# Two last groups of a four-layer graph network by halves, and a planner's costs for small GpSimd operations and loads

## The chip, the cores and the metric

The kernel runs on one core of a Trainium2 chip. The core has five engines that run side by side, each with a queue of its own which it works off in order: TensorE (PE, matmuls), VectorE (DVE), ScalarE (ACT), GpSimd (POOL) and SyncE (SP, which here only starts transfers). The metric is the time of one execution on the device in microseconds; the median of several runs stands for a kernel.

## What is computed

128 graphs of 64 nodes with 256 features each pass four layers. Each layer normalises its input, applies ReLU, runs a graph operation and adds the result to x.

```python
def layer0(h):                       # graph convolution twice, then LSTMs over windows of nodes
    h = relu(adj @ (h @ Wg0 + bg0)); h = relu(adj @ (h @ Wg1 + bg1))
    for p in 1, 2, 3, 4:             # windows of p nodes; the last node of each takes the LSTM's state
        last = lstm_last(Wih[p-1], Whh[p-1], bih[p-1], bhh[p-1], windows(h, p))
        h = h.at[:, arange(64 // p) * p + p - 1].set(last)
    return h
def layer1(x, L):                    # L scaled by its largest eigenvalue; attention; MLP
    x1 = relu(layernorm((L_norm @ x) @ Wc + bc, g1, be1)) + x
    x2 = layernorm(x1 + attention(x1, Wq, Wk, Wv) @ Wo + bo, g2, be2)
    return layernorm(x2 + gelu(x2 @ W1 + b1) @ W2 + b2, g3, be3)
def layer2(h):                       # graph attention: e[i,j] = leaky_relu(s1[i] + s2[j])
    Wh = h @ W; e = leaky_relu((Wh @ a1)[:, :, None] + (Wh @ a2)[:, None, :], 0.2)
    return softmax(where(adj == 0, -inf, e)) @ Wh
def layer3(f):                       # U: eigenvectors of the normalised Laplacian (eigh)
    h = relu((U.T @ f) @ W1 + b1)
    return U @ (h @ W2 + b2)
for layer in layers: x = x + layer(relu(layernorm(x)))
```

## The kernel before

Rows of x (128 graphs x 64 nodes) are cut into 64 tiles of 128 rows, two graphs in each. Layer 0 works on 8 groups of 8 tiles and writes its result to a scratch array in DRAM (`put`). Layers 1 to 3 work on 16 groups of 4 tiles (`HT = 4`), which the loop at the end of the kernel fetches from there (`fetch`), passes through `layer1`, `layer2`, `layer3` and stores by two tiles. The eigenvectors are computed beside layer 0 by a long row of small operations on 64 partitions, mostly on VectorE.

No instruction is issued as it is written. `plan.proxy` records each call as an `Op` with the engine, its dependencies, and a cost and latency by formula (`cost`); `Plan.schedule` then goes through time: at each step it takes the operation that can start first, gives it a buffer from a pool (`big`, `stat`, `bank` and others) and advances its engine's clock, and `Plan.issue` emits everything in the order found. So all instructions of the profile have one line, L347, that of the emitting loop, and groups are told apart by the names of tiles. A tile's name is that of the memory it was given: `sums`, `mids`, `arena`, `Wih` and `Whh` are reused as working buffers once their first use is over. The planner's clock shapes the order alone; on the chip an instruction starts when its semaphores allow.

What the change touches in the planner:

- In `record`, `op.port` marks operations [...] all of GpSimd's, and VectorE's with all operands in SBUF that are no reductions or statistics.
- In `cost`, the branch for `"G"` gives a GpSimd operation its duration: a power 0.44 + 0.14 n us, others 0.12 + 0.00218 n, where n is the elements of a partition.
- In `schedule`, the clock `port` is held for the operation's whole cost, and no operation with `op.port` may start in the plan before it is free. A dependent operation is ready at the end of the one before it plus `slack`: 0.4 us for a TensorE operation of the later layers, 0.12 for other TensorE operations, 0.05 otherwise.
- `rank` orders what could start at once. The last six groups share one rank level and then go by group and by the length of the path behind them.

Of the layers, these steps recur in the argument. `ln_stats` takes statistics of each tile on VectorE (`bn_stats`, `bn_aggr`), then four GpSimd operations on 128x4 values, one of them the power -0.5. `relu_norm` applies them on ScalarE, tile by tile. `mix` multiplies each tile's two graphs by a 64x64 matrix with small matmuls into two banks, which ScalarE copies out (`mix_fm`). `layer2` forms the scores from two weighted sums (`scalar_tensor_tensor` with `accum_out`), a matmul that spreads s2 over rows (`s2d`), six steps on 128x256 values, an exponential, a transpose, the mix by the attention, the product by `W2a` and a scaled add to x. `layer3` mixes by `Ub`, multiplies by `W3a`, takes the maximum with the negated bias, mixes by `UTb`, adds `C3`, multiplies by `W3b` and adds to x.

Of the kernel before, what the change touches and what calls it, by code (L numbers as in the profile page):

```python
# [12 lines left out]
N = 64  # L13
# [55 lines left out]
class Plan:  # L69
# [44 lines left out]
    def record(self, eng, name, args, kw):  # L114
# [42 lines left out]
        if op is self.run:  # L157
# [5 lines left out]
                                 and all(str(ap.space) == "SB" for ap in flat))  # L163
        op.index = len(self.ops)
# [14 lines left out]
    def cost(op, aps):  # L179
# [39 lines left out]
        if op.eng == "G":  # L219
            c = 0.44 + 0.14 * n if op.kw.get("op") is ALU.pow else 0.12 + 0.00218 * n  # L220
            return c, c + 0.05
# [8 lines left out]
    def schedule(self):  # L230
# [20 lines left out]
        while len(order) < len(self.ops):  # L251
# [42 lines left out]
            if op.port:  # L294
                port = t + cost
# [13 lines left out]
            for o in op.after:  # L309
                o.wait -= 1  # L310
                if o.eng != e:
                    o.ready = max(o.ready, end + self.slack(o))
                else:
                    o.ready = max(o.ready, end - 0.01 if op in o.late and e != "PE" else t + cost)
                if not o.wait:
                    ready[o.eng].append(o)
# [577 lines left out]
P = 128  # L894
# [116 lines left out]
def gnn_kernel(ctx: ExitStack, tc: tile.TileContext, a, out):  # L1011
# [54 lines left out]
    def bank(name):  # L1066
        return plan.value("bank")
# [541 lines left out]
    def relu_norm(x):  # L1609
        sc, bi = ln_stats(x)  # L1610
        h = tm()
        for t in range(HT):
            ACT.activation(h[:, t, :], x[:, t, :], AF.Relu, scale=sc(t), bias=bi(t))
        return h

    def mix_fm(h, m):

        dst = fm()
        for i, ps in enumerate(mix(lambda t, c: h[:, t, tok(c)], m, HT)):
            evac(dst.rearrange("p c (t b n) -> p c t b n", t=HT, b=2)[:, :, :, i, :], ps, 1)  # L1620
        return dst
# [76 lines left out]
    def layer2(x):  # L1698


        h = relu_norm(x)
        big, stat = plan.value("big"), plan.value("stat")
        s12 = stat[:, 2 * HT:4 * HT].rearrange("p (k t) -> p k t", k=2)
        for k in range(2):
            for t in range(HT):
                V.scalar_tensor_tensor(big[:, t * D:(t + 1) * D], h[:, t, :], 1.0, wa[:, k, :], op0=ALU.mult, op1=ALU.mult, accum_out=s12[:, k, t:t + 1])

        s2d, s1m, e2, e = (big[:, i * HT * N:(i + 1) * HT * N].rearrange("p (t n) -> p t n", n=N) for i in range(4))
        V.tensor_mul(s2d, vec(ident2), s12[:, 1, :].unsqueeze(2).to_broadcast([P, HT, N]))
        G.tensor_add(s1m, vec(mask2), s12[:, 0, :].unsqueeze(2).to_broadcast([P, HT, N]))  # L1710
        ps = bank("s2")[:, :HT * N]
        PE.matmul(ps, same, flat(s2d), start=True, stop=True)
        V.tensor_add(flat(e), ps, flat(s1m))
        V.tensor_scalar(e2, e, 0.2, None, op0=ALU.mult)
        V.tensor_max(e, e, e2)
        softmax_shift(e, stat[:, :HT])
        attn = plan.value("attn").rearrange("p (t k) -> p t k", t=HT)
        for i in range(2):
            r = half(i)
            ACT.activation(attn[r, :, r], e[r], AF.Exp)  # L1720
        ssum = stat[:, HT:2 * HT]
        V.reduce_sum(ssum, attn, axis=AX.X)
        V.reciprocal(ssum, ssum)
        pT = plan.value("big")[:, :HT * P]
        evac(pT, transposes([attn[:, t, :] for t in range(HT)]), 1)
        aT = mix_fm(h, lambda t: pT[:, tok(t)])
        for t0 in (0, 2):
            ps = proj_tm(lambda c, t: aT[:, c, tok(t)], W2a, 2, t0)
            for t in (t0, t0 + 1):
                V.scalar_tensor_tensor(x[:, t, :], ps[:, (t - t0) * D:(t - t0 + 1) * D], ssum[:, t:t + 1], x[:, t, :], op0=ALU.mult, op1=ALU.add)  # L1730

    def layer3(x):
        h = relu_norm(x)
        for t0 in (0, 2):
            G.tensor_add(x[:, t0:t0 + 2, :], x[:, t0:t0 + 2, :], vec(b3b, 2))
        aT = mix_fm(h, lambda t: Ub)
        hid = tm(HT, P)
        ps = bank("hid")
        for t in range(HT):
            for c in range(2):  # L1740
                PE.matmul(ps[:, tok(t)], aT[:, c, tok(t)], W3a[:, c, :], start=c == 0, stop=c == 1)
        V.tensor_tensor(hid, ps.rearrange("p (t f) -> p t f", t=HT), vec(nb3a), op=ALU.max)
        uT = tm(HT, P)
        for i, ps in enumerate(mix(lambda t, c: hid[:, t, :], lambda t: UTb, HT, 1)):
            V.tensor_tensor(uT.rearrange("p t (b n) -> p t b n", b=2)[:, :, i, :], ps[:, 0], vec(C3[:, half(i)]), op=ALU.add)
        for t0 in (0, 2):
            ps = proj_tm(lambda c, t: uT[:, t, :], W3b.unsqueeze(1), 1, t0)
            V.tensor_add(pair(x, t0), ps, pair(x, t0))

    for g in range(NT // HT):  # L1750
        plan.group = REST + g
        x = fetch(put[g // 2][:, g % 2 * HT:(g % 2 + 1) * HT])
        layer1(x)
        layer2(x)
        layer3(x)
        for t0 in range(0, HT, 2):
            SP.dma_start(xout[g][:, t0:t0 + 2, :], x[:, t0:t0 + 2, :])
# [54 lines left out]
```

## Time and profile before

| | us |
|---|---|
| median of 3 runs | 2116.32 |
| lowest, highest | 2113.99, 2117.18 |
| the profiled execution | 2117.02 |
| its span, first to last instruction | 2115.2 |
| mean granted TensorE clock | 0.997 |
| 256 KB stores, issue to landing (median) | 2.6 |
| 512 KB fetches from `put` to `big` (median) | 6.4 |

In the profile, PE is the matmul stream and PEld the loading of its weights; a float32 matmul leaves two MATMUL and two LDWEIGHTS records. A line of a timeline gives start, duration, engine, line, operation, output and inputs, shapes, how many equal instructions were merged (x4), and in brackets how long the engine had been idle before and what released it. The granted clock is TensorE's, 1.00 at full speed. In time the stages lie so: layer 0 with the eigenvectors up to about 1240 us, a change-over in which its last group and the first groups of the later layers run together, then the later layers, the last six groups interleaved.

### The profile page before, as it was taken

What the parts mean: (1) busy time and instruction counts of PE and PEld (TensorE: products, weight loads), DVE (VectorE), ACT (ScalarE), POOL (GpSimd) and SP (SyncE); (2) the same over time, 40 slices, a digit from 0 to 9 for tenths busy, and PEclk for the clock granted to TensorE, in tenths of its full rate; (3) what the DMA queues carried; (4) which work ended last, traced back from release to release, by engine and by line L of the source; (5) the groups of instructions that cost most, each with busy time, mean ns of one, the idle gap of its engine ahead of it and who ended that gap; (6) DMA issues with size and microseconds to landing.
All of it is one profiled execution on the core that took longest, in us unless ns stands there. A gap on an engine that the chain in (4) does not pass through costs nothing.

```text
span 2115.2 us, 48093 instructions
## 1 busy us (share of the span) xinstructions
PE 2072.3 (98%) x17924; PEld 1675.9 (79%) x17924; DVE 1767.0 (84%) x6669; ACT 1094.7 (52%) x2451; POOL 756.6 (36%) x1144
## 2 busy tenths in 40 slices
PE   8999999999999999999999999999999999999997
PEld 6688689688788788788788789877778778877775
DVE  7788888889999999999988956868779699885785
ACT  3344544534543543543444345666666567575763
POOL 6522212222201201201100215685467658663452
PEclk9999999999999999999999999999999999999999
DMA  6000100100100100100000211100000000000001
GB/s 229 1 3 13 52 3 2 62 2 2 60 1 1 61 1 2 46 1 10 32 1 21 90 49 35 62 1 22 22 21 22 21 22 22 22 2 11 1 12 51
DMA packets 44875, 57.83 MB, mean 27 GB/s; under 512 B 8929, under 2 KB 38497, under 8 KB 44641
## 3 DMA queue, kind: packets, MB, share of 16 engines
q1 hardware_dynamic: 43536, 53.71, 7.9%
q8 instruction: 141, 2.31, 0.5%
q10 hardware_dynamic: 1104, 1.05, 0.2%
q14 instruction: 94, 0.76, 0.1%
HBM read 37.53 MB, written 16.78 MB: 26 GB/s over the span
## 4 chain that ended last, share of the span: by engine, by line
PE 80%; DVE 13%; issue 2%; ACT 2%; POOL 2%; DMA 0%; SPq 0%; ACTq 0%; DVEq 0%; POOLq 0%
PE bank L347 64%; PE seed L347 16%; DVE arena L347 5%; DVE big L347 4%; DVE stat L347 2%; ACT mids L347 1%; DVE mids L347 1%; POOL stat L347 1%; DVE sums L347 1%; POOL big L347 1%; ACT big L347 0%; DMA arena<-put 0%; DVE bank L347 0%; POOL sums L347 0%; DVE seed L347 0%
## 5 line engine op out<-in xcount | busy, mean ns | idle before, releaser
L347 PE MATMUL bank<-big,Wih 128*128 128x512 f32 (+4 forms) x1802 | 554.5, 424 | 2.9 <-DVE big L347 1.9
L347 PEld LDWEIGHTS bank<-big,Wih 128*128 128x128 f32 x1802 | 314.7, 190 | 145.5 <-issue 95.5
L347 PE MATMUL bank<-big,sums 128*128 128x128 f32 (+3 forms) x2328 | 375.7, 289 | 5.2 <-DVE seed L347 2.5
L347 ACT ACTIVATE mids<-bank,bl 128x512 f32<-128x512 f32 (+2 forms) x432 | 247.2, 576 | 214.3 <-PE bank L347 195.2
L347 PEld LDWEIGHTS bank<-big,sums 128*128 128x128 f32 (+1 forms) x2328 | 298.5, 180 | 42.8 <-issue 19.6
L347 PE MATMUL bank<-big,Whh 128*128 128x128 f32 (+3 forms) x1294 | 312.3, 327 | 0.0
L347 DVE TENSOR_TENSOR arena<-arena 64x42 f32<-64x42 f32 (+6 forms) x1358 | 276.5, 231 | 18.4 <-POOL arena L347 1.2
L347 PEld LDWEIGHTS bank<-big,Whh 128*128 128x128 f32 x1294 | 214.0, 191 | 18.5 <-issue 10.5
L347 ACT ACTIVATE mids<-seed,bl 128x256 f32<-128x256 f32 (+2 forms) x192 | 102.0, 531 | 217.0 <-PE seed L347 209.0
L347 DVE TENSOR_TENSOR big<-mids 128x512 f32<-128x512 f32 (+2 forms) x256 | 151.1, 597 | 27.1 <-ACT mids L347 17.1
L347 POOL TENSOR_SCALAR stat<-stat 128x4 f32<-128x4 f32 (+1 forms) x228 | 68.4, 301 | 281.1 <-DVE stat L347 268.9
L347 PE MATMUL seed<-big,sums 128*128 128x128 f32 (+3 forms) x896 | 143.3, 291 | 0.0
L347 DVE SCALAR_TENSOR_TENSOR arena<-arena 64x1 f32<-64x1 f32 (+15 forms) x565 | 136.1, 264 | 4.5 <-POOL arena L347 1.0
L347 POOL TENSOR_TENSOR big<-big 128x128 f32<-128x128 f32 (+2 forms) x55 | 32.9, 600 | 294.6 <-DVE big L347 151.7
L347 POOL TENSOR_TENSOR stat<-stat,mhalf 128x4 f32<-128x4 f32 (+1 forms) x114 | 123.9, 1087 | 4.8
L347 ACT COPY seed<-bank 128x128 f32<-128x128 f32 (+2 forms) x192 | 54.0, 281 | 135.8 <-PE bank L347 128.5
L347 ACT ACTIVATE mids<-big 128x256 f32<-128x256 f32 (+2 forms) x176 | 89.5, 511 | 66.3 <-DVE big L347 62.1
L347 ACT COPY mids<-bank 128x256 f32<-128x256 f32 (+3 forms) x290 | 94.8, 352 | 51.9 <-PE bank L347 51.5
L347 PEld LDWEIGHTS seed<-big,sums 128*128 128x128 f32 (+1 forms) x896 | 118.4, 183 | 3.5 <-issue 0.3
L347 DVE TENSOR_SCALAR arena<-arena 64x1 f32<-64x1 f32 (+10 forms) x506 | 100.4, 206 | 7.8 <-POOL arena L347 0.5
L347 DVE TENSOR_TENSOR big<-big,mids 128x256 f32<-128x256 f32 (+2 forms) x196 | 99.0, 509 | 7.0 <-ACT mids L347 6.0
L347 PE MATMUL bank<-Wih,big 128*128 128x256 f32 x408 | 104.8, 383 | 0.0
(517 smaller groups left out, 4480.4 us busy)
## 6 DMA issues: line engine op xcount, KB each, us to landing
big<-in_x_dram SPq DMA_DIRECT2D x29, 512.0 KB, 5.0
put<-big SPq DMA_DIRECT2D x15, 512.0 KB, 3.2
big<-put SPq DMA_DIRECT2D x8, 512.0 KB, 6.4
out_dram<-big SPq DMA_DIRECT2D x16, 256.0 KB, 2.6
Wih<-in_WihT_dram SPq DMA_DIRECT2D x3, 1024.0 KB, 11.4
Whh<-in_WhhT_dram SPq DMA_DIRECT2D x3, 1024.0 KB, 12.9
arena<-put SPq DMA_DIRECT2D x3, 512.0 KB, 5.9
sums<-put SPq DMA_DIRECT2D x3, 512.0 KB, 4.3
```

The costliest lines, as they stand in the source:

```text
L347: getattr(self.engines[op.eng], name)(*map(real, args), **{k: real(a) for k, a in kw.items()})
```

## The change

`layer2` and `layer3` take a step: 4 tiles as before for the first 14 groups, 2 tiles for the last two. With a step of 2 each passes through its whole row of operations for tiles 0 and 1 and again for tiles 2 and 3, in shared buffers (`h`, `aT` and others) but with statistics and score values of its own. In the planner three costs change: an operation whose operands all have two dimensions and at most 64 elements in a row holds the port for 0.06 us instead of its whole cost; a GpSimd operation of at most 64 elements other than a power costs 0.2 us; and whatever depends on a transfer that SP started is held ready 1.5 us later. These three bear on the order of the whole kernel.

```diff
@@ -161,6 +161,8 @@
 
         op.port = eng == "G" or (eng == "V" and not name.startswith("bn_") and "reduce" not in name
                                  and all(str(ap.space) == "SB" for ap in flat))
+        wide = max(ap.ap[-1][1] if len(ap.ap) == 2 else 65 for ap in flat) > 64
+        op.hold = op.cost if wide else 0.06
         op.index = len(self.ops)
         self.ops.append(op)
         self.link(op)
@@ -217,7 +219,7 @@
                 c += 0.12
             return c, c + 0.15
         if op.eng == "G":
-            c = 0.44 + 0.14 * n if op.kw.get("op") is ALU.pow else 0.12 + 0.00218 * n
+            c = 0.44 + 0.14 * n if op.kw.get("op") is ALU.pow else 0.12 + 0.00218 * n if n > 64 else 0.2
             return c, c + 0.05
         c = max(0.6, free(aps[0]) * aps[0].ap[0][1] * 4e-6 / 0.39)
         return c, c + 2.2
@@ -292,7 +294,7 @@
                 many, cost, lat = op.many, cost + 0.178, lat + 0.178
             now[e] = t + cost
             if op.port:
-                port = t + cost
+                port = t + min(cost, op.hold)
             end = t + lat
             for v in op.vals:
                 if v.buf is None:
@@ -309,7 +311,7 @@
             for o in op.after:
                 o.wait -= 1
                 if o.eng != e:
-                    o.ready = max(o.ready, end + self.slack(o))
+                    o.ready = max(o.ready, end + self.slack(o) + (1.5 if e == "SP" else 0.0))
                 else:
                     o.ready = max(o.ready, end - 0.01 if op in o.late and e != "PE" else t + cost)
                 if not o.wait:
@@ -1606,18 +1608,19 @@
         V.reduce_max(mx, s, axis=AX.X)
         V.tensor_sub(s, s, mx.unsqueeze(2).to_broadcast(list(s.shape)))
 
-    def relu_norm(x):
-        sc, bi = ln_stats(x)
-        h = tm()
-        for t in range(HT):
-            ACT.activation(h[:, t, :], x[:, t, :], AF.Relu, scale=sc(t), bias=bi(t))
+    def relu_norm(x, h=None, t0=0, n=HT):
+        h = tm() if h is None else h
+        sc, bi = ln_stats(x[:, t0:t0 + n], n)
+        for t in range(n):
+            ACT.activation(h[:, t0 + t, :], x[:, t0 + t, :], AF.Relu, scale=sc(t), bias=bi(t))
         return h
 
-    def mix_fm(h, m):
-
-        dst = fm()
-        for i, ps in enumerate(mix(lambda t, c: h[:, t, tok(c)], m, HT)):
-            evac(dst.rearrange("p c (t b n) -> p c t b n", t=HT, b=2)[:, :, :, i, :], ps, 1)
+    def mix_fm(h, m, dst=None, t0=0, n=HT):
+
+        dst = fm() if dst is None else dst
+        part = dst[:, :, t0 * P:(t0 + n) * P].rearrange("p c (t b n) -> p c t b n", t=n, b=2)
+        for i, ps in enumerate(mix(lambda t, c: h[:, t0 + t, tok(c)], lambda t: m(t0 + t), n)):
+            evac(part[:, :, :, i, :], ps, 1)
         return dst
 
     def layer1(x):
@@ -1695,64 +1698,70 @@
             V.tensor_mul(x2[:, t0:t0 + 2, :], x2[:, t0:t0 + 2, :], vec(g3, 2))
             V.tensor_add(x[:, t0:t0 + 2, :], x[:, t0:t0 + 2, :], x2[:, t0:t0 + 2, :])
 
-    def layer2(x):
-
-
-        h = relu_norm(x)
-        big, stat = plan.value("big"), plan.value("stat")
-        s12 = stat[:, 2 * HT:4 * HT].rearrange("p (k t) -> p k t", k=2)
-        for k in range(2):
-            for t in range(HT):
-                V.scalar_tensor_tensor(big[:, t * D:(t + 1) * D], h[:, t, :], 1.0, wa[:, k, :], op0=ALU.mult, op1=ALU.mult, accum_out=s12[:, k, t:t + 1])
-
-        s2d, s1m, e2, e = (big[:, i * HT * N:(i + 1) * HT * N].rearrange("p (t n) -> p t n", n=N) for i in range(4))
-        V.tensor_mul(s2d, vec(ident2), s12[:, 1, :].unsqueeze(2).to_broadcast([P, HT, N]))
-        G.tensor_add(s1m, vec(mask2), s12[:, 0, :].unsqueeze(2).to_broadcast([P, HT, N]))
-        ps = bank("s2")[:, :HT * N]
-        PE.matmul(ps, same, flat(s2d), start=True, stop=True)
-        V.tensor_add(flat(e), ps, flat(s1m))
-        V.tensor_scalar(e2, e, 0.2, None, op0=ALU.mult)
-        V.tensor_max(e, e, e2)
-        softmax_shift(e, stat[:, :HT])
-        attn = plan.value("attn").rearrange("p (t k) -> p t k", t=HT)
-        for i in range(2):
-            r = half(i)
-            ACT.activation(attn[r, :, r], e[r], AF.Exp)
-        ssum = stat[:, HT:2 * HT]
-        V.reduce_sum(ssum, attn, axis=AX.X)
-        V.reciprocal(ssum, ssum)
-        pT = plan.value("big")[:, :HT * P]
-        evac(pT, transposes([attn[:, t, :] for t in range(HT)]), 1)
-        aT = mix_fm(h, lambda t: pT[:, tok(t)])
-        for t0 in (0, 2):
-            ps = proj_tm(lambda c, t: aT[:, c, tok(t)], W2a, 2, t0)
-            for t in (t0, t0 + 1):
-                V.scalar_tensor_tensor(x[:, t, :], ps[:, (t - t0) * D:(t - t0 + 1) * D], ssum[:, t:t + 1], x[:, t, :], op0=ALU.mult, op1=ALU.add)
-
-    def layer3(x):
-        h = relu_norm(x)
-        for t0 in (0, 2):
-            G.tensor_add(x[:, t0:t0 + 2, :], x[:, t0:t0 + 2, :], vec(b3b, 2))
-        aT = mix_fm(h, lambda t: Ub)
-        hid = tm(HT, P)
-        ps = bank("hid")
-        for t in range(HT):
-            for c in range(2):
-                PE.matmul(ps[:, tok(t)], aT[:, c, tok(t)], W3a[:, c, :], start=c == 0, stop=c == 1)
-        V.tensor_tensor(hid, ps.rearrange("p (t f) -> p t f", t=HT), vec(nb3a), op=ALU.max)
-        uT = tm(HT, P)
-        for i, ps in enumerate(mix(lambda t, c: hid[:, t, :], lambda t: UTb, HT, 1)):
-            V.tensor_tensor(uT.rearrange("p t (b n) -> p t b n", b=2)[:, :, i, :], ps[:, 0], vec(C3[:, half(i)]), op=ALU.add)
-        for t0 in (0, 2):
-            ps = proj_tm(lambda c, t: uT[:, t, :], W3b.unsqueeze(1), 1, t0)
-            V.tensor_add(pair(x, t0), ps, pair(x, t0))
+    def layer2(x, step):
+
+        h, big, attn = tm(), plan.value("big"), plan.value("attn").rearrange("p (t k) -> p t k", t=HT)
+        pT, aT = plan.value("big")[:, :HT * P], fm()
+        for t0 in range(0, HT, step):
+            n, ts = step, slice(t0, t0 + step)
+            relu_norm(x, h, t0, n)
+            stat = plan.value("stat")
+            s12 = stat[:, 2 * HT:2 * HT + 2 * n].rearrange("p (k t) -> p k t", k=2)
+            for k in range(2):
+                for t in range(n):
+                    V.scalar_tensor_tensor(big[:, (t0 + t) * D:(t0 + t + 1) * D], h[:, t0 + t, :], 1.0, wa[:, k, :], op0=ALU.mult, op1=ALU.mult, accum_out=s12[:, k, t:t + 1])
+
+            s2d, s1m, e2, e = (big[:, (t0 * 4 + i * n) * N:(t0 * 4 + (i + 1) * n) * N].rearrange("p (t n) -> p t n", n=N) for i in range(4))
+            V.tensor_mul(s2d, vec(ident2, n), s12[:, 1, :].unsqueeze(2).to_broadcast([P, n, N]))
+            G.tensor_add(s1m, vec(mask2, n), s12[:, 0, :].unsqueeze(2).to_broadcast([P, n, N]))
+            ps = bank("s2")[:, :n * N]
+            PE.matmul(ps, same, flat(s2d), start=True, stop=True)
+            V.tensor_add(flat(e), ps, flat(s1m))
+            V.tensor_scalar(e2, e, 0.2, None, op0=ALU.mult)
+            V.tensor_max(e, e, e2)
+            softmax_shift(e, stat[:, :n])
+            for i in range(2):
+                r = half(i)
+                ACT.activation(attn[r, ts, r], e[r], AF.Exp)
+            ssum = stat[:, HT:HT + n]
+            V.reduce_sum(ssum, attn[:, ts], axis=AX.X)
+            V.reciprocal(ssum, ssum)
+            pt = bank("tr")
+            for t in range(n):
+                PE.transpose(pt[:, tok(t)], attn[:, t0 + t, :], ident)
+            evac(pT[:, t0 * P:(t0 + n) * P], pt[:, :n * P], 1)
+            mix_fm(h, lambda t: pT[:, tok(t)], aT, t0, n)
+            for u0 in range(t0, t0 + n, 2):
+                ps = proj_tm(lambda c, t: aT[:, c, tok(t)], W2a, 2, u0)
+                for t in (u0, u0 + 1):
+                    V.scalar_tensor_tensor(x[:, t, :], ps[:, (t - u0) * D:(t - u0 + 1) * D], ssum[:, t - t0:t - t0 + 1], x[:, t, :], op0=ALU.mult, op1=ALU.add)
+
+    def layer3(x, step):
+        h, aT, hid, uT = tm(), fm(), tm(HT, P), tm(HT, P)
+        for t0 in range(0, HT, step):
+            n, ts = step, slice(t0, t0 + step)
+            relu_norm(x, h, t0, n)
+            for u0 in range(t0, t0 + n, 2):
+                G.tensor_add(x[:, u0:u0 + 2, :], x[:, u0:u0 + 2, :], vec(b3b, 2))
+            mix_fm(h, lambda t: Ub, aT, t0, n)
+            ps = bank("hid")
+            for t in range(n):
+                for c in range(2):
+                    PE.matmul(ps[:, tok(t)], aT[:, c, tok(t0 + t)], W3a[:, c, :], start=c == 0, stop=c == 1)
+            V.tensor_tensor(hid[:, ts], ps[:, :n * P].rearrange("p (t f) -> p t f", t=n), vec(nb3a, n), op=ALU.max)
+            for i, ps in enumerate(mix(lambda t, c: hid[:, t0 + t, :], lambda t: UTb, n, 1)):
+                V.tensor_tensor(uT[:, ts].rearrange("p t (b n) -> p t b n", b=2)[:, :, i, :], ps[:, 0], vec(C3[:, half(i)], n), op=ALU.add)
+            for u0 in range(t0, t0 + n, 2):
+                ps = proj_tm(lambda c, t: uT[:, t, :], W3b.unsqueeze(1), 1, u0)
+                V.tensor_add(pair(x, u0), ps, pair(x, u0))
 
     for g in range(NT // HT):
         plan.group = REST + g
         x = fetch(put[g // 2][:, g % 2 * HT:(g % 2 + 1) * HT])
         layer1(x)
-        layer2(x)
-        layer3(x)
+        step = 2 if g >= NT // HT - 2 else HT
+        layer2(x, step)
+        layer3(x, step)
         for t0 in range(0, HT, 2):
             SP.dma_start(xout[g][:, t0:t0 + 2, :], x[:, t0:t0 + 2, :])
     plan.issue()
```

## The prediction

> **What bounds the kernel now.** I read the page first (busy shares, slices), then busy time by stage, then the timeline of the last chain, then the releasers.
>
> ```profile
> span 2115.2 us, 48093 instructions
> PE 2072.3 (98%) x17924; PEld 1675.9 (79%) x17924; DVE 1767.0 (84%) x6669; ACT 1094.7 (52%) x2451; POOL 756.6 (36%) x1144
> PE   8999999999999999999999999999999999999997
> ```
>
> TensorE is busy 98%, and its slices are all nines but the first and the last. So only its idle time, 2115.2 - 2072.3 = 42.9 us, and work done at a lowered clock can be won. Where that lies, the busy time by stage says (columns: stretch, length, then busy time and count of each engine, granted clock, DMA share, GB/s):
>
> ```profile
> 0.00:16.00 16.00, 12.28 (x92) 10.45 (x96) 9.61 (x62) 5.10 (x9) 7.01 (x29) 0.79 0.81 255
> 106.00:1216.00 1110.00, 1104.84 (x7637) 902.18 (x7636) 1004.83 (x4403) 506.36 (x1297) 196.66 (x369) 1.00 0.07 22
> 1216.00:1428.00 212.00, 204.45 (x1843) 180.30 (x1842) 143.27 (x398) 120.81 (x270) 112.08 (x149) 1.00 0.12 36
> 1428.00:2062.00 634.00, 625.58 (x7009) 496.53 (x7007) 507.54 (x1449) 412.80 (x767) 368.83 (x502) 1.00 0.05 17
> 2062.00:2092.45 30.45, 24.29 (x422) 20.83 (x423) 22.90 (x75) 13.13 (x27) 11.05 (x17) 1.00 0.16 54
> 2092.45:2111.40 18.95, 13.01 (x173) 9.88 (x171) 7.87 (x21) 3.15 (x6) 4.18 (x6) 0.83 0.09 29
> 2111.40:2115.20 3.80, 0.00 (x0) 0.00 (x0) 0.69 (x1) 0.00 (x0) 0.00 (x0) 0.94 0.42 138
> ```
>
> TensorE idles 3.7 us up to 16, 5.2 in the 1110 us of layer 0, 7.6 where layer 0 gives way to the later layers, 8.4 in the next 634, then 6.2 in 30, 5.9 in 19, and 3.8 at the very end, where one add and the stores are left. The remaining 2.1 lies between 16 and 106. The end is the dense place, and its chain is one group's layer 3, every step on four tiles:
>
> ```profile
> 2092.22 1.66 DVE L347 SCALAR_TENSOR_TENSOR big<-bank,stat,big 128x256 f32<-128x256 f32 x4 [2.10 <-PE bank L347]
> 2093.80 1.39 DVE L347 BATCH_NORM_STATS2 stat<-big 128x6 f32<-128x256 f32 x4
> 2095.87 1.04 POOL L347 TENSOR_TENSOR stat<-stat,mhalf 128x4 f32<-128x4 f32 x1
> 2097.53 2.07 ACT L347 ACTIVATE sums<-big,stat 128x256 f32<-128x256 f32 x4 [10.44 <-POOL stat L347]
> 2103.57 2.05 PE L347 MATMUL bank<-Whh,sums 128*128 128x128 f32 x16 [1.17 <-ACT sums L347]
> 2105.66 0.69 DVE L347 TENSOR_TENSOR big<-bank,Whh 128x512 f32<-128x512 f32 x1 [3.79 <-PE bank L347]
> 2110.25 1.06 PE L347 MATMUL bank<-Wih,big 128*128 128x256 f32 x2
> 2111.42 0.69 DVE L347 TENSOR_TENSOR big<-bank,big 128x512 f32<-128x512 f32 x1 [0.16 <-PE bank L347]
> ```
>
> The reader is to see a relay: each engine waits for the one before (ScalarE 10.44 us), and little else is left to fill the gaps. The last matmuls take 1.06 us for two records, where 0.59 is usual: the mean clock of this stretch is 0.83.
>
> [...] Over all VectorE tensor_tensor, scalar_tensor_tensor and tensor_scalar instructions without PSUM that started while a GpSimd operation ran: beside a wide one 345, of which 204 ran over the median of their shape by more than 150 ns, 110.6 us in all; beside a power (-0.5 on 128x4 and the like) 151, of which 6, 4.2 us; beside another small one 107, of which 2, none in sum. One place shows it:
>
> ```profile
> 1452.18 0.68 DVE L347 TENSOR_TENSOR arena<-arena,Whh 128x512 f32<-128x512 f32 x1
> 1452.43 1.33 POOL L347 TENSOR_TENSOR stat<-stat,mhalf 128x4 f32<-128x4 f32 x1
> 1452.78 1.28 DVE L347 TENSOR_TENSOR big<-big,arena 128x512 f32<-128x512 f32 x2
> ```
>
> Two adds with both inputs in SBUF, under a power, take 0.64 each; the power is what is stretched (1.04 alone). [...] an add takes 0.69 us at 128x512, 0.41 at 128x256, 0.29 at 128x128. [...] half clock from 2098.2 to 2101.6 and again from 2108.4 to 2111.8, each after some 3.4 us with a third or so of work. [...] VectorE is busy 7.87 of 18.95 us at the end[...].
>
> **Part 1: halves in the last two groups.** The instruction order after the change has 2 matmuls more (9250 to 9252), 22 VectorE instructions, 14 of ScalarE and 18 of GpSimd; table loads stay at 41. TensorE's work is thus unchanged. At the end, four half groups take turns where two groups did: after the last layer-2 product, some 9 us of matmuls (at full clock) remain in both orders.
>
> From that product's end (2092.45) to the last matmul's (2111.31) there are 18.9 us before. For the last half, step by step: scaled adds 4 to 2, 0.87 (two such elsewhere); statistics 1.67 to 0.96 (two of each, 0.73 and 0.23); GpSimd 1.94 to 1.61 (the power on 128x2 takes 0.71, on 128x4 1.04); ReLU 2.07 to 1.09; hand-overs between these 0.45. Sum 5.0. Then the mix by U 0.9 to 0.45; wait and evacuation 1.67 to 1.2 (copies of 128x256 at 0.37, of 128x512 at 0.59); W3a 2.05 to 1.05; its maximum with hand-overs 0.88 to 0.6; the second mix 0.55 to 0.35; the biases 0.95 to 0.7; W3b 3.36 to 1.3 (two matmuls: 0.9 at full clock, 1.7 at half). Sum 10.6. The 1.4 us in which the mix waited for the other group's product (2099.60 to 2101.00) become a sharing: 9 us of matmuls stand in these 10.6, so I add 1 to 3. That gives 11.6 to 13.6 for 18.9: a gain of 5.3 to 7.3, and I take 6.3. Some 2.9 of it is half clock, which two windows of 3.4 us cost when matmuls fill them.
>
> Price of the extra instructions: for each group some 1.7 us of VectorE (layer 2's six 128x256 steps 6 x (2 x 0.29 - 0.41) = 1.0; layer 3's maximum and biases 0.5; sums and reciprocals 0.2), 3.4 in all. They lie in the last 100 us; VectorE has 7.5 us free after 2062. I count 0; without that cover, +3.4. Before 2092 the halves may also thin out the 6.2 us of idle time: 0 taken, from -2 to +2. The stores are by two tiles already; after the last add (2112.1) the end is as before, 3.1 us.
>
> **Part 2: the schedule's hold.** The planner reserved VectorE's port for a power's whole 0.58 to 1.0 us; 187 of these and 411 other small operations stood in the plan as stalls that the trace does not have. Now they hold 0.06. Nothing runs faster; the order moves on every engine. By that order the eigenvector work is ahead by up to 30 us of matmuls in layer 0, and U is written at matmul 4320 instead of 4343. As a measure of risk I count TensorE's waits whose latest dependency on TensorE lies less than 1.5 us of its stream back: layer 0, 345 before, 341 after; the change-over, 79 and 70; the later layers up to the end, 15 and 18. Behind stream position 2030, those under 0.5 us fall from 8 to 4. So neither gain nor loss can be read for the middle: I take -0.5. Bounds: a third of the 23.3 us idle between 16 and 2062 gained (-8), or VectorE's lost reserve showing as stalls (+12, rival below).
>
> **Part 3: loads have 1.5 us more.** At the start VectorE's queue held an add on adj ahead of the first group's statistics:
>
> ```profile
> 3.86 0.43 DVE L347 BATCH_NORM_STATS2 stat<-big 128x6 f32<-128x256 f32 x1
> 5.70 0.22 DVE L347 TENSOR_TENSOR arena<-adj,adjT 64x64 f32<-64x64 f32 x1 [1.41 <-DMA adj<-in_adj_dram]
> 5.84 0.17 DVE L347 BATCH_NORM_AGGREGATE stat<-stat 128x2 f32<-128x6 f32 x1
> ```
>
> In the new order the statistics go first, so up to 1.4 us goes. But the row sum of adj now stands behind seven of eight tiles' statistics (about 8 x 0.49 us), at some 8.3 us, and the matmul that reads it stands ahead of the first mix (9.22 before). So that is next late: I take -0.5, from -1.5 to +1. Elsewhere a load ended one VectorE wait of 1.6 us. SP's queue has the same 197 transfers in nearly the same order; the later ones are merely waited for later, at no cost.
>
> **Sum.** The profiled execution took 2117.02 us (span 2115.2 and 1.8 around it). 2117.0 - 6.3 - 0.5 - 0.5 = 2109.7. That execution lies 0.7 above the median of the runs (2116.32), so I forecast 2109.0.
>
> **The rivals.** A difference under 0.2% (4.2 us) cannot be told from none.
> *Given back*: the end shrinks, but the new order loses about as much elsewhere, or VectorE, full from 2062 to 2078 (16.0 of 16), makes the halves late by its 3.4 us of extra work. For it: 3.4 is half the gain, and every order is new. Against: the counts above. 2116.3 - 6.3 + 5 = 2115 (2112 to 2120). Chance 0.18.
> *Slower*: in layer 0 VectorE is busy 1004.8 of 1110. The plan's false stalls were a reserve against the true ones beside wide operations (110.6 us, single ones up to 2.7). Without it, matmuls are placed right when a result is due. Were one in ten of the 345 close waits to stall 0.5 us, that is 17 us: 2116.3 - 7 + 17 = 2126. It decides from about 11 us of new idle time between 16 and 2062, half as much again as there is. For it: 90% busy. Against: close waits are as many as before. Chance 0.13.
> *More*: the truer plan also takes a third of the middle's idle time: 2109 - 8 = 2101 (2097 to 2104.5). For it: 7.6 us idle in the change-over, with VectorE at 143 of 212. Chance 0.09.
> That the new hold misstates the chip would be a further one; the counts beside powers exclude it.
>
> **How the numbers follow.** The forecast has 0.60, own range 2104.5 to 2112.5, of which 0.01 is above 2112.1. Faster by over 0.2%: 0.59 + 0.09 = 0.68; within: 0.01 + 0.18 = 0.19; slower: 0.13. A range from 2102 to 2119 leaves out most of *slower* and half of *more*, together below 0.2.
>
> **What would show it.** Right: between the last layer-2 product and the last matmul about 12 to 13 us instead of 18.9, mean clock there over 0.83, TensorE's idle time from 16 to 2062 still about 23 us. The first mix before 9.2. Wrong: that idle time above 30 or below 17, a last chain of over 16 us, or TensorE's busy sum outside the end changed by more than 2 us.

## The result and the profile after

| | before | after |
|---|---|---|
| median, us | 2116.32 | 2101.82 |
| lowest, highest | 2113.99, 2117.18 | 2099.95, 2104.41 |
| span of the profiled execution | 2115.2 | 2098.2 |
| TensorE idle in it (span less busy) | 42.9 | 33.0 |

The ratio is 0.9931, interval 0.9917 to 0.9946: the change is 14.5 us faster, twice the 7.3 of the forecast. The head of the changed kernel's page:

```profile
span 2098.2 us, 48166 instructions
PE 2065.2 (98%) x17928; PEld 1678.8 (80%) x17928; DVE 1767.8 (84%) x6691; ACT 1097.0 (52%) x2465; POOL 777.8 (37%) x1162
PE   8999999999999999999999999999999999999998
```

TensorE has 4 more of its 17928 matmul records and is busy 7.1 us less. Busy time by stage of the changed kernel follows (columns as before). The end came 16 to 17 us sooner; the last stretches are shifted by as much, so that they lie as far from the last matmul as those shown of before.

```profile
0.00:16.00 16.00, 12.74 (x107) 11.38 (x108) 9.74 (x64) 6.93 (x13) 8.50 (x34) 0.82 0.81 245
106.00:1216.00 1110.00, 1103.40 (x7573) 902.36 (x7571) 1014.74 (x4413) 504.73 (x1292) 208.14 (x370) 1.00 0.07 22
1216.00:1428.00 212.00, 207.48 (x1909) 181.96 (x1908) 138.50 (x354) 121.17 (x267) 107.48 (x142) 1.00 0.13 38
1428.00:2046.00 618.00, 612.10 (x6838) 493.13 (x6837) 493.26 (x1435) 408.21 (x761) 372.69 (x506) 1.00 0.05 16
2046.00:2076.00 30.00, 25.51 (x455) 21.34 (x454) 29.28 (x114) 16.93 (x39) 17.13 (x29) 1.00 0.17 55
2076.00:2094.40 18.40, 17.18 (x266) 14.15 (x264) 11.59 (x37) 7.12 (x19) 7.91 (x15) 1.00 0.22 73
```

Idle time in the 1110 us of layer 0 rose from 5.2 to 6.6, in the change-over it fell from 7.6 to 4.5. Between 2076 and the last matmul 1.2 us are idle in 18.4, where 5.9 of 18.95 were, and the clock stays at 1.00. VectorE is nearly full before that: 29.28 of 30. The last chain, as the timeline of the changed kernel gives it:

```profile
2081.56 1.89 PE L349 MATMUL bank<-Wih,mids 128*128 128x256 f32 x8
2083.49 0.88 DVE L349 SCALAR_TENSOR_TENSOR sums<-bank,stat,sums 128x256 f32<-128x256 f32 x2 [1.15 <-PE bank L349]
2084.28 0.74 DVE L349 BATCH_NORM_STATS2 stat<-sums 128x6 f32<-128x256 f32 x2
2085.77 0.72 POOL L349 TENSOR_TENSOR stat<-stat,mhalf 128x2 f32<-128x2 f32 x1
2087.11 1.10 ACT L349 ACTIVATE sums<-sums,stat 128x256 f32<-128x256 f32 x2 [1.81 <-POOL stat L349]
2089.96 1.05 PE L349 MATMUL seed<-Whh,sums 128*128 128x128 f32 x8
2091.05 0.42 DVE L349 TENSOR_TENSOR mids<-seed,Whh 128x256 f32<-128x256 f32 x1
2093.13 1.13 PE L349 MATMUL bank<-Wih,arena 128*128 128x256 f32 x4 [0.86 <-DVE arena L349]
2094.37 0.69 DVE L349 TENSOR_TENSOR sums<-bank,sums 128x512 f32<-128x512 f32 x1 [1.29 <-PE bank L349]
```

Every step stands on two tiles (x2, x8, x4). Most take about half of what they took; the GpSimd power takes 0.72 us where it took 1.04, and the last add, which stood on two tiles already, 0.69 as before. From the end of the last layer-2 product (2083.45) to the last matmul's (2094.26) there are 10.8 us instead of 18.9. The same product now ends 9.0 us earlier as well. That is the part for which the forecast had 1.0.

To find where those 9 us come from, I lined up both kernels by TensorE's work instead of by time: each matmul counts with the usual duration of its shape, and the table further down says how much later or earlier the same amount of work is reached than in the kernel before. These lags are estimates: another weight for the many 64x64 matmuls moves them by 1 to 3 us, and by more where a long wait lies near. The changed kernel is 4.2 us late at the end of layer 0, 2.6 early after the change-over and 7.6 early at 2000 us of work (of 2039).

### The profile page after: what moved, and what is told of

Read it like the earlier page. It is cut to its first block, busy times and chain, and to the rows that moved or that the text cites. A ratio compares the mean times of both kernels' runs of the same rounds, so it can differ in the third digit from the quotient of the medians.

```text
span 2098.2 us, 48166 instructions
## 1 busy us (share of the span) xinstructions
PE 2065.2 (98%) x17928; PEld 1678.8 (80%) x17928; DVE 1767.8 (84%) x6691; ACT 1097.0 (52%) x2465; POOL 777.8 (37%) x1162
## 4 chain that ended last, share of the span: by engine, by line
PE 87%; DVE 10%; issue 1%; ACT 1%; POOL 0%; DMA 0%; DVEq 0%; ACTq 0%
PE bank L349 70%; PE seed L349 17%; DVE big L349 3%; DVE arena L349 3%; DVE stat L349 2%; DVE mids L349 1%; ACT mids L349 1%; DVE sums L349 1%; DMA big<-in_x_dram 0%; DVE seed L349 0%; POOL stat L349 0%; DVE Whh L349 0%; ACT big L349 0%; DVE bank L349 0%; DMA adjT<-in_adjT_dram 0%
## 5 line engine op out<-in xcount | busy, mean ns | idle before, releaser
L349 PE MATMUL bank<-big,sums 128*128 128x128 f32 (+3 forms) x1936 | 361.5, 301 | 5.8 <-DVE big L349 2.5
L349 PE MATMUL bank<-big,Whh 128*128 128x128 f32 (+3 forms) x1304 | 322.5, 333 | 1.4 <-ACT big L349 1.4
L349 PEld LDWEIGHTS bank<-big,sums 128*128 128x128 f32 (+1 forms) x1936 | 286.5, 188 | 40.8 <-issue 17.7
L349 DVE SCALAR_TENSOR_TENSOR arena<-arena 64x1 f32<-64x1 f32 (+16 forms) x565 | 128.7, 251 | 10.6 <-ACT arena L349 3.5
L349 POOL TENSOR_TENSOR big<-big,B1T 128x512 f32<-128x512 f32 x32 | 37.8, 1186 | 255.1 <-DVE big L349 233.8
L349 ACT COPY mids<-bank 128x256 f32<-128x256 f32 (+3 forms) x320 | 107.6, 357 | 38.7 <-PE bank L349 36.8
L349 POOL MEMSET arena<- 64x2 f32 (+5 forms) x72 | 7.8, 113 | 306.2 <-DVE arena L349 301.7
L349 DVE TENSOR_SCALAR arena<-arena 64x1 f32<-64x1 f32 (+8 forms) x506 | 102.3, 211 | 6.8 <-POOL arena L349 0.3
L349 PE MATMUL seed<-big,Whh 128*128 128x128 f32 (+3 forms) x424 | 103.6, 326 | 0.3 <-DVE big L349 0.3
## 6 DMA issues: line engine op xcount, KB each, us to landing
Whh<-in_WhhT_dram SPq DMA_DIRECT2D x3, 1024.0 KB, 13.6
```

The costliest lines, as they stand in the source:

```text
L349: getattr(self.engines[op.eng], name)(*map(real, args), **{k: real(a) for k, a in kw.items()})
```

## The experiments

Undoing the three planner costs and the step gives exactly the order of the kernel before, so each part can be tried alone. "Whole groups" means the step of 4 in all groups, "full set" all three costs. The kernel before, run again beside each set of experiments, took 2116.3 to 2116.8, and each ratio is taken to the runs beside it. The theories, by the letters of the expectations: A, the parts add up; B, any new order moves the time by several us, whatever its cause; C, the parts need each other; L, the room for loads pays alone; and from e5 on A', the three costs together make a truer plan, which pays whatever order comes of it.

**The parts alone.** e1 has the halves with the costs of before; e2, e3 and e4 have whole groups with the short hold, the room for loads, and all three costs.

```diff
 e1:  three planner costs as before, step = 2 if g >= NT // HT - 2 else HT
 e2:  -port = t + cost                     +port = t + min(cost, op.hold)
 e3:  -end + self.slack(o)                 +end + self.slack(o) + (1.5 if e == "SP" else 0.0)
 e4:  all three costs of the change, step = HT
```

> The planner's costs as before; layers 2 and 3 of the last two groups by halves. Theory A (the parts add up: the end gains by halves, the middle by the truer hold): about 9 us under the kernel before, all of it after 2050; up to there the same order and times as before. Theory B (any new order moves the time by several us): the end still gains 6 to 9, but as the last groups interleave with four others, stretches before 2050 move too. Theory C (the three parts need each other): under 3 us.

> Only the hold of the port: 0.06 us for small operations; costs of GpSimd, loads and steps as before. Theory A: 5 to 8 us under the kernel before, in the change-over and the later layers (1216 to 2062), with the end as before. Theory B: anything within +-6 us, with no tie to places where small GpSimd operations lie. Theory L (it is the room for loads that pays): within 2 us of before.

> Only the 1.5 us more for what depends on a transfer of SP. Theory A: within 2 us of before, the first 20 us about 1 us later. Theory L: 5 to 8 us under before, in the change-over and later, where weights and tiles are fetched. Theory B: anything within +-6 us.

> All three planner costs, whole groups to the end. Theory A: 7 to 8 us under before (what the changed kernel gained up to the last 60 us), the last 40 us as long as before. Theory B: may stand far from the sum of the single parts, by 4 us or more. Theory C: under 3 us.

Measured: e1 2113.55 us (ratio 0.9984, 0.9977 to 0.9991), e2 2126.7 (1.0042), e3 2131.83 (1.0072), e4 2107.64 (0.9958, 0.9943 to 0.9973). Two of the costs lose 10 and 15 us alone, and all three together gain 9: A, C and L fall, and B, which had at most 6 us for e2 and e3, had its spread too small. On top of all three the halves are worth 2107.64 - 2101.82 = 5.8 us; with the costs of before they are worth 3. The chain itself shrank in both cases: from the last layer-2 product to the last matmul it takes 18.9 us before, 12.2 in e1, 18.2 in e4 and 10.8 in the changed kernel. So in e1 some of the gain is lost ahead of it: from 1428 to 2046 TensorE idles 11.0 us in e1 and 6.7 before. Two stretches show it. First the kernel before, then e1:

```profile
1960.00:1990.00 30.00, 30.00 (x188) 21.63 (x188) 20.70 (x71) 22.91 (x38) 12.96 (x21) 1.00 0.01 2
2010.00:2030.00 20.00, 20.00 (x202) 14.44 (x201) 16.26 (x52) 13.61 (x25) 10.46 (x14) 1.00 0.00 1
```

```profile
1960.00:1990.00 30.00, 28.46 (x357) 21.15 (x359) 19.00 (x57) 23.55 (x39) 12.59 (x19) 1.00 0.01 2
2010.00:2030.00 20.00, 18.92 (x197) 14.00 (x195) 15.38 (x54) 12.01 (x21) 14.24 (x21) 1.00 0.01 2
```

TensorE had no idle time in these two stretches and has 2.6 us with the halves. The first holds 357 matmul records instead of 188, many small ones, so the order there is another; that these are the halves' own matmuls, planned among the other groups, fits but was not tried alone. The end gives the loss back and more.

And e4, the new plan without halves, has the old relay at its end. Its last two stretches by stage:

```profile
2046.00:2076.00 30.00, 24.48 (x420) 20.96 (x424) 29.86 (x90) 13.05 (x26) 13.51 (x20) 1.00 0.11 37
2076.00:2105.10 29.10, 19.72 (x319) 15.74 (x308) 12.03 (x29) 7.26 (x14) 7.37 (x11) 0.89 0.22 74
```

TensorE is idle 9.4 of the last 29.1 us, and the clock is reduced again (0.89). In the changed kernel the stretch from 2076 to the last instruction is 22.2 us long and has 5.0 idle.

**Is it the truth of the costs, or the order they happen to give?** e5 and e6 shift the room for loads a little with the full set; e7 gives the kernel before a very small room; e8 leaves the room out of the full set.

```diff
 e5:  -(1.5 if e == "SP" else 0.0)   +(1.4 if e == "SP" else 0.0)      full set, step = HT
 e6:  -(1.5 if e == "SP" else 0.0)   +(1.7 if e == "SP" else 0.0)      full set, step = HT
 e7:  -end + self.slack(o)           +end + self.slack(o) + (0.1 if e == "SP" else 0.0)   only this
 e8:  -+ (1.5 if e == "SP" else 0.0)                                   full set, step = HT
```

> As the planner-only kernel, with 1.4 us for loads instead of 1.5: no cost of the chip is better or worse met, but the order changes. Theory B (the gain of the middle is one order's luck): may lie 4 us or more from that kernel's 2107.6, on either side. Theory A' (the three costs together make a truer plan, which pays whatever the order): within 3 us of 2107.6, and at any rate under the kernel before.

> As the planner-only kernel, with 1.7 us for loads. As for 1.4: theory B, 4 us or more from 2107.6; theory A', within 3 us of it and under the kernel before.

> The kernel before with 0.1 us for loads and nothing else: too little to be room for anything. Theory B: the order changes all the same, and the time moves by 4 us or more. Theory A': within 3 us of the kernel before.

> The hold of 0.06 us and the 0.2 us for small GpSimd operations, without the room for loads. Theory A': with both costs of GpSimd nearer the chip the time is under the kernel before, by up to 9 us. Theory B: anything from -9 to +15 us, as the single parts showed.

Measured: e5 2101.13 (0.9928, 0.9913 to 0.9943), e6 2104.2 (0.9944), e7 2118.9 (1.0012), e8 2119.99 (1.002). A tenth or two of a microsecond in one cost moves the time by 2.6 to 6.5 us, so the order does matter by itself. B had asked for 4 us or more: e5 has it (6.5), e6 (3.4) and e7 (2.6) have not. A' had asked for 3 or less, and for a gain in e8: only e7 fits. Yet all three full sets stay 9 to 15 us ahead, and without the room the gain is gone. That still looked like a truer plan.

**The other combinations, and the best version.** f1 is the changed kernel with 1.4 for 1.5. f2 gives the kernel before 1.4 us of room alone; f3 and f4 leave one cost out of the full set.

```diff
 f1:  -(1.5 if e == "SP" else 0.0)   +(1.4 if e == "SP" else 0.0)      all else as changed, halves too
 f2:  the same 1.4, the other two costs as before                      step = HT
 f3:  -0.12 + 0.00218 * n if n > 64 else 0.2   +0.12 + 0.00218 * n     hold and 1.5 kept, step = HT
 f4:  -port = t + min(cost, op.hold)           +port = t + cost        0.2 and 1.5 kept, step = HT
```

> The changed kernel whole, with 1.4 us in place of 1.5 us of room for loads. Theory A' (the three costs together make a truer plan, whatever order comes of it; the halves are worth what they were worth in the changed kernel against the same costs with whole groups, 5.8 us): 2101.1 - 5.8 = 2095.3, from 2093 to 2098. Theory B (each order is a draw with a spread of several us): anywhere from 2094 to 2106, so a time above 2099 speaks for B.

> The kernel before with 1.4 us of room for loads and nothing else. A': room for loads pays only beside the other two costs, so it stays slower than before, 2118 to 2132. If 1.4 us is itself the better value, whatever stands beside it: under 2112. B: anywhere from 2112 to 2132.

> The kernel before with the short hold and 1.5 us of room for loads, without the 0.2 us for small GpSimd operations (theirs stays at 0.12 to 0.26). A' (room for loads and the short hold carry the gain; 0.2 for 0.13 us changes little in the plan): 2104 to 2111. B: anywhere from 2101 to 2132; over 2114 says that a change of 0.07 us in the cost of small operations decides over more than 6 us, which no cause in the plan's truth could explain.

> The kernel before with the 0.2 us for small GpSimd operations and 1.5 us of room for loads, without the short hold. A' (without the hold the plan keeps its false stalls): not faster than before by more than 3 us, so over 2113. B: anywhere from 2101 to 2132; under 2110 says that the hold isn't needed for the gain.

Measured: f1 2094.34 (0.9898, 0.988 to 0.9915), f2 2136.2 (1.0098), f3 2133.94 (1.0085), f4 2134.49 (1.0085). f1 beats both kernels, in the range of A' (2093 to 2098), and against e5 the halves are worth 6.8 us. f2, f3 and f4 lie 2 to 4 us above even the range of B. The page of f1:

```profile
span 2091.7 us, 48181 instructions
PE 2061.3 (99%) x17928; PEld 1677.0 (80%) x17928; DVE 1760.7 (84%) x6691; ACT 1097.4 (52%) x2465; POOL 776.7 (37%) x1162
PE   9999999999999999999999999999999999999998
```

f3 is the blow to the truer plan: taking 0.2 us back to 0.12 to 0.26 for small GpSimd operations, at most 0.08 us for each, costs 26 us against e4. It made me compare the orders themselves. Counting VectorE's instructions that stand in the same sequence for 25 and more, e4, e5, e6, f1 and the changed kernel share 69 to 100% of their order between 1420 and 1750 us, and those with the same step 83 to 97% after that. So they are one draw there, not five, and the two pairs for the halves (e4 to after, e5 to f1) are one pair of orders measured twice. What sets e5 and e6 apart from e4 is in place by 1200 us of work (table below), ahead of this common order. e7 shares 98 to 100% with the kernel before, and e1 all of it up to 1750 us; the others share at most a tenth with either from 1420 us on.

**The same plans with a new order.** g and h break this: a change of 2 ns (or 0.5 ns) in one cost of the plan, made alike in the full set and in the kernel before, all with whole groups.

```diff
 g1, g2:  -c = 0.07 + 0.00082 * n ...      +c = 0.072 + 0.00082 * n ...     ScalarE; full set, before
 g3, g4:  -c = 0.075 + 0.00105 * n         +c = 0.077 + 0.00105 * n         VectorE; full set, before
 h1, h2:  -c = 0.001672 * n + 0.006 ...    +c = 0.001672 * n + 0.0065 ...   TensorE; full set, before
```

> The three planner costs with whole groups, and 2 ns more in the plan for each ScalarE operation: no statement about the chip worth naming, but in the plan the order of the later layers comes out quite another (runs of 25 and more VectorE operations in the same sequence fall there from 83 to 97% between the earlier variants of these costs to some 30% and less). A' (the costs make a truer plan, whatever order comes of it): 2100 to 2110, as with the other three. B (an order is a draw, and the four good ones shared one draw in the later layers): no more than a draw from 2100 to 2136, likely above 2112.

> The kernel before with the same 2 ns for each ScalarE operation. A': about 2116, from 2112 to 2120. B: a draw from 2100 to 2136; above 2122 says that the order of the kernel before was itself a good draw.

> The three planner costs with whole groups, and 2 ns more in the plan for each general VectorE operation. A': 2100 to 2110. B: a draw from 2100 to 2136, likely above 2112.

> The kernel before with the same 2 ns for each general VectorE operation. A': about 2116, from 2112 to 2120, and above g3 by 6 to 15. B: a draw from 2100 to 2136, in no fixed order to g3.

> The three planner costs with whole groups, and 0.5 ns more in the plan for each wide matmul. A' as first stated fell with the two pairs before (2126.4 and 2125.0 with all three costs, where it said 2100 to 2110). B (an order is a draw; the orders of before and of the changed kernel were good ones): 2116 to 2136. C' (a draw, but the three costs shift the draws down by some 6 us, the mean of the two pairs, 8.5 and 3.3): 2119 to 2130, and below h2 by 2 to 10.

> The kernel before with the same 0.5 ns for each wide matmul. B: 2116 to 2136, in no fixed order to h1. C': 2124 to 2137, above h1 by 2 to 10.

Measured, full set against before: 2126.36 against 2134.89, 2125.03 against 2128.32, 2122.97 against 2122.93. All six are slower than the kernel before (ratios 1.0025 to 1.0086). The truer plan as I had stated it (2100 to 2110) fell in all three. Half a nanosecond to two in one planned cost took 15 to 19 us from e4. C', a shift of the draws by 2 to 10 us, came from the first two pairs (8.5 and 3.3 us) and fell in the third, which has none; whether a smaller shift remains is open.

The table puts all kernels side by side. "Half clock" is the time in which TensorE was granted half its clock, in stretches that begin after the first 60 us, up to the last matmul. The last three columns are the lag against the kernel before (us, negative is earlier) at 1200, 1400 and 2000 us of matmul work: end of layer 0, after the change-over, before the end. All columns from TensorE's idle time on are of the one profiled execution, which lies up to 3.1 us under its kernel's median (e3; 2.8 in e5).

| kernel | costs | median | TensorE idle | half clock | 1200 | 1400 | 2000 |
|---|---|---|---|---|---|---|---|
| before | old | 2116.3 | 42.9 | 6.3 | 0 | 0 | 0 |
| e1 (halves) | old | 2113.6 | 40.7 | 0 | 0.0 | -0.5 | 4.8 |
| after (halves) | full | 2101.8 | 33.0 | 0 | 4.2 | -2.6 | -7.6 |
| e4 | full | 2107.6 | 39.5 | 2.4 | 3.7 | -3.1 | -6.9 |
| e5 | full | 2101.1 | 36.3 | 0 | -4.2 | -10.2 | -14.4 |
| e6 | full | 2104.2 | 38.1 | 0 | 0.4 | -6.4 | -9.7 |
| f1 (halves) | full | 2094.3 | 30.4 | 3.4 | -3.9 | -10.2 | -15.4 |
| g1 | full, 2 ns | 2126.4 | 47.0 | 17.1 | 5.2 | -0.8 | 13.4 |
| g3 | full, 2 ns | 2125.0 | 45.1 | 6.8 | 3.8 | -2.2 | 11.3 |
| h1 | full, 0.5 ns | 2123.0 | 45.7 | 6.8 | 6.7 | 2.9 | 10.1 |
| g2 | old, 2 ns | 2134.9 | 52.9 | 23.9 | 5.0 | 8.7 | 19.8 |
| g4 | old, 2 ns | 2128.3 | 49.6 | 6.8 | 9.3 | 6.3 | 12.1 |
| h2 | old, 0.5 ns | 2122.9 | 49.7 | 3.4 | 10.2 | 9.7 | 8.7 |
| e7 | loads 0.1 | 2118.9 | 42.4 | 0 | 4.5 | 3.7 | 3.3 |
| e2 | hold | 2126.7 | 48.1 | 16.0 | 6.8 | 5.2 | 9.3 |
| e3 | loads 1.5 | 2131.8 | 52.2 | 3.4 | 7.0 | 8.7 | 16.3 |
| f2 | loads 1.4 | 2136.2 | 51.8 | 10.1 | 8.3 | 10.8 | 20.6 |
| e8 | hold, small | 2120.0 | 45.4 | 0 | 6.8 | 5.9 | 5.1 |
| f3 | hold, loads | 2133.9 | 54.5 | 10.2 | 7.4 | 5.2 | 18.2 |
| f4 | small, loads | 2134.5 | 52.4 | 20.5 | 13.8 | 12.9 | 20.8 |

Three things stand in it. In the change-over (1400 less 1200) all eight full sets gain, 3.8 to 6.8 us; the others lie between -3.0 and +3.7. In each of the three pairs the full set gains more there (by 9.7, 3.0 and 3.3 us). That is the one place where the three costs look like a cause, though several of these orders are alike there as well. The idle time from 1216 to 1428 us is a weaker witness: 3.7 to 5.1 us in the eight full sets, 7.1 to 10.5 in most others, but 4.6 in e7, which differs from the kernel before by 0.1 us in one cost, and 4.9 and 5.0 in f3 and g4. So it is not shown. In the later layers (2000 less 1400) the shared order of the full sets gains 3 to 5 us, but g1, g3 and h1, with the same costs in another order, lose 7 to 14. And the kernel before is itself a good draw: no whole-group kernel without the full set comes under it, and at 1200 us of work all are later but e1, e5 and f1. In e3, f2, f4, g4, h1 and h2 4 to 8 us of that lag is there after the first 60 us of work already, while loads still arrive; e5 and f1 are 4 us early there.

**What a bad order looks like.** g1 and e4 have the same costs but for 2 ns and are 2 us apart at 1400 us of work. Busy time by stage, first e4, then g1:

```profile
1430.00:1460.00 30.00, 30.00 (x214) 26.49 (x213) 24.68 (x79) 22.11 (x45) 22.64 (x33) 1.00 0.00 1
```

```profile
1430.00:1460.00 30.00, 24.32 (x143) 17.19 (x143) 17.02 (x42) 14.90 (x27) 20.69 (x24) 0.83 0.01 1
1447.70:1457.90 10.20, 7.46 (x78) 6.00 (x79) 5.24 (x8) 7.44 (x14) 6.75 (x8) 0.50 0.01 2
```

The timeline of g1 there:

```profile
1443.30 2.85 POOL L349 TENSOR_TENSOR sums<-sums,Wih 128x512 f32<-128x512 f32 x2
1443.48 0.59 PE L349 MATMUL bank<-Whh,sums 128*128 128x256 f32 x2
1443.66 1.36 DVE L349 TENSOR_TENSOR arena<-ident,stat 128x256 f32<-128x256 f32 x1
1445.07 0.70 PE L349 MATMUL bank<-arena,same 128*128 128x256 f32 x2 [1.00 <-DVE arena L349]
1448.07 0.84 ACT L349 ACTIVATE Wih<-arena 64x256 f32<-64x256 f32 x2 [6.27 <-DVE arena L349]
1448.96 1.11 PE L349 MATMUL bank<-ident,Wih 128*128 128x128 f32 x4 [3.19 <-ACT Wih L349]
1451.04 1.99 PE L349 MATMUL bank<-mids,sums 64*64 64x64 f32 x64 [0.96 <-ACT mids L349]
```

This is layer 2's score chain of one group with no other group's matmuls placed into it: the multiply by s2, the spreading matmul, the six steps on VectorE, the exponential, the transpose, the copy, the mix. VectorE's multiply is drawn out to 1.36 us beside two wide GpSimd operations (0.41 is the median of its kind in this kernel). TensorE waits 1.00, 3.19 and 0.96 us and works 0.7 of some 4.9 us. Within the second wait, at 1447.7, its clock falls to half for 10.2 us, in which 7.46 us of matmuls are worth 3.7; of the 3.4 us before the fall it had worked 0.70. So one missed filling cost about 5 us of waiting and nearly 4 of clock, where e4 has 30.00 us busy of 30. That is near half of the 18 us by which g1 falls behind e4 between 1400 and 2000 us of work; the others were not followed up.

In two pairs the same two sums explain most of the difference. Changed against before: idle -9.9, half clock -3.2 (half the matmul time at half clock after 60 us), together -13.1 of -17.0 in span. g2 against before: +10.0 and +8.1 of +19.3. Elsewhere they explain about half or less: e5 against before -9.8 of -18.7, g3 +2.5 of +7.7. What is left shows mostly as busy time at full clock (-4.0 in the changed kernel, -7.6 in e5). Part of that is waits again: a matmul record that starts after TensorE stood still adds on average 0.25 us more busy time than one of its shape in a full stream. Such starts number 53 at full clock before (13.5 us in sum), 42 in the changed kernel (10.6) and 38 in e5 (9.9). For the rest, with matmul ends modelled, the records do not say whether it is shorter waits or weight loads.

## Why the prediction was right and wrong

*The end by halves, -6.3: right in size, for one order.* Measured 5.8 (e4 to after) and 6.8 (e5 to f1). The chain took 10.8 us, just below the 11.6 to 13.6: its first half, to the end of the ReLU, was 4.8 where 5.0 was worked out, and from there to the last matmul 6.0 against 5.6. The 1 to 3 us added for the sharing of TensorE with the other half thus came to 0.2. With the old costs the halves gave only 3 (e1), though the chain shrank there as well (to 12.2): what the rest of the order loses, taken as nothing, was real there, with 2.6 us of idle time around 1960 to 2030 as a part of it. The clock's share of the gain was in part chance: e4 and e5 run the same relay, and e4 loses 1.2 us to half clock in it, e5 nothing, as the clock fell 2.4 us before the last matmul in one and 2.6 after it in the other. The forecast's reading that a third or so of work stood in the 3.4 us before each fall of the clock holds for the first (1.19 us); for the second it was half (1.77).

*The start, -0.5: wrong in sign, at the edge of its bound.* The row sum did move behind the tiles' statistics (8.88 us, 8.3 forecast), and what was named as next late became late. First before, then after:

```profile
6.50 0.22 DVE L347 TENSOR_REDUCE rscol<-adj 128x1 f32<-128x64 f32 x1 [0.18 <-DMA adj<-in_adj_dram]
9.22 1.41 PE L347 MATMUL bank<-adjTb,mids 64*64 64x64 f32 x32 [1.96 <-ACT mids L347]
```

```profile
8.88 0.18 DVE L349 TENSOR_REDUCE rscol<-adj 128x1 f32<-128x64 f32 x1
9.12 0.43 PE L349 MATMUL bank<-adjT,rscol 64*128 64x64 f32 x2 [1.54 <-DVE rscol L349]
11.13 0.92 PE L349 MATMUL bank<-adjTb,mids 64*64 64x64 f32 x24 [0.69 <-ACT mids L349]
```

The mixes start at 9.48 instead of 9.22 and then wait once more for ScalarE's tiles. At 20 us of work the kernel is about 1.1 us late (bound +1).

*The middle, -0.5: the step that failed.* "Neither gain nor loss can be read for the middle" became a term of -0.5. The planner costs together, start included, are worth 8.7 us (before to e4) where 1.0 stood. In the profiled executions it is 10.4 at the last matmul: by the lag of e4 6.9 us by 2000 us of work, with a start that loses 0.7 of it, and 3.5 in the last 39, where the old relay comes out with less half clock (2.4 us for 6.3). It was no failure to see the idle time: that of 16 to 2062 went from 23.3 to 20.2 at the matching point, inside what was called right. The test of "busy sum outside the end changed by more than 2 us" was the one that spoke: 7.1 us less busy in all, of which 3.2 is the half clock of the end; the 4 that remain are at full clock. So TensorE's busy time, which the forecast took as fixed but for the clock, is not. The count of close waits fell in the change-over (79 to 70) and rose later (15 to 18); idle time fell in both (7.6 to 4.5; 8.4 to 5.9 at the matching point). What the runs put in its place is not a mechanism of the costs but a spread: whole-group kernels of nearly equal plans lie between 2101 and 2136 us. What in an order makes it good stays open. The forecast gave the middle a range from -8 to +12 and then took its centre near zero with a chance of 0.60 within 4 us; the spread measured over whole-group orders goes from -15 (e5) to +20 (f2), mostly on the slow side. By these runs it was luck that the changed kernel fell on the fast side.

*The rivals.* "More" has the sum (2101) and the place (the change-over, 7.6 to 4.5 idle), but not the account: the middle's idle time fell by 3.1, not by a third (8), and the rest came from a longer gain at the end and from busy time. Its reason, the truer plan, is not shown either: it holds for the change-over at best. "Slower" is what most other orders did: at 1200 us of work 15 of the 19 are 3.7 to 13.8 us late, 4.2 in the changed kernel. Its reason, layer 0 losing its reserve, is not shown: six of them lost 4 to 8 us in the first 60 us, and idle time from 106 to 1216 is 5.1 to 9.4 in all. VectorE full before the end, the ground for "given back", came true (29.28 of 30) without holding up the last chain.

## What to carry to other kernels

Where a planner orders thousands of instructions on engines that are 84 to 98% busy, a change of any planned cost is first of all a new draw, here from a spread of 35 us in 2116; judge such a cost by several orders with and without it, each disturbed by a nanosecond or two, and keep the best order, but don't read the one result as proof of the cost. Work on the chain that ends the kernel (10.6 us by its steps, 10.8 measured) can be forecast step by step from the profile; what the order before it gains or loses cannot (the halves' net is 3 to 7 us), so its range has to be that of the draws. In looking for what makes a draw bad, look for one group's chain left alone on TensorE for 3 to 5 us: in g1 it cost about 5 us of waiting and nearly 4 more in clock.

## What the runs showed of the hardware

Half clock came on top of waits. In g1 10.2 us of it began within the second of two waits (1.00 and 3.19 us), and the kernels with the most of it (f4 20.5, g2 23.9) are among the slowest (2134.5 and 2134.9 us). In the changed kernel there is none from 17.2 us to the last matmul; the end of before lost 3.2 us to it.

In these traces the clock fell after stretches in which TensorE was partly busy. It changed on a grid of 3.4 us (half-clock stretches of 3.4, 6.8 and 10.2 us). In the 20 traces, after the first 60 us, all 28 steps of this grid that went ahead of a fall from full to half clock had TensorE busy, by its matmul records, for 12 to 64% of their time. No step under 43% was followed by full clock; from there to 64% both occurred. In the kernel before, 34% of the step were busy ahead of the fall at 2098.2, with no single wait over 2.2 us, and 52% ahead of the one at 2108.4, while the step from 1425.7, with 53%, was followed by full clock.
